# A graph-attention layer in fp32: the second projection with two levels of Strassen's scheme

## Chip, cores, metric

One core of one Trainium2 chip. Times are device microseconds of a whole execution. TensorE is PE in the profile, VectorE is DVE, ScalarE is ACT, GpSimd is POOL, and SP issues most transfers.

## The reference

128 graphs of 64 nodes with 512 features, all fp32: a norm with ReLU, a four-head graph attention, a second attention over the joined heads, a feed-forward network, a second norm and the residual.

```python
h = jnp.maximum(_layernorm(x), 0.0)
# attention 1: 4 heads, softmax over the neighbours, ELU; heads joined to 2048 features
h = elu(_gat_heads(h, adj, W_heads, a_heads));  h = transpose+reshape to [B, N, 2048]
# attention 2: the "second projection" is h @ W_out, 2048 -> 512
out = elu(_gat_heads(h, adj, W_out[None], a_out[None])[:, 0])
y = relu(out @ w1 + b1) @ w2 + b2 + out
return x + layernorm(y) * gamma + beta
```

## The kernel before

The 8192 rows go in 16 groups of four tiles of 128 rows. In each group TensorE does the first projection of one group (`g_a`, four heads), then its second projection (`g_b`), into which everything else is interleaved: the first attention of the next group (`pz`), the feed-forward products of the group before (`g_c` with w1, `g_d` with w2), transposes and scores. All four products use one level of Strassen's scheme in Winograd's form: seven products of half-size blocks instead of eight, numbered 1 to 7, which add up in three PSUM banks. A list scheduler fixes the order of each engine's instructions when the kernel is built; at run time each engine works through its own queue.

```python
ps = ctx.enter_context(tc.tile_pool(name="ps", bufs=6, space=PSUM))    # "mm" banks; 2 more for "aux"

def unit(name, product, post, order):
    own = {1: 1, 2: 1, 5: 5, 3: 5, 6: 6, 7: 6, 4: 6}       # which bank a product adds to
    def after(p):                                          # what happens when product p is done
        if p in (1, 5, 6):
            if p == 6:
                nc.vector.tensor_tensor(gb[6], gb[6], sb["s1"], ALU.add)
            nc.scalar.copy(sb[nm], gb[p])                  # s1, s5, t: copies of the banks
        elif p == 2: post("c11", gb[1])
        elif p == 7: post("c22", gb[6], sb["s5"], gb[1])
        elif p == 3: post("c12", gb[5], sb["t"], gb[5])
        else:        post("c21", gb[6])
    ...
```

So product 2 may start only when the copy s1 of product 1 is made, because it adds to the same bank; 7 waits in the same way for 6, and 4 for c22, which reads the bank after 7.

```python
def norm1(t):                                              # X[t] was loaded into another buffer
    mean, rstd = norm_stats(X[t], "n1", t)                 # VectorE, GpSimd
    HN[t] = big.tile([P, F], FP, tag="hn", name=f"hn{t}", bufs=G)
    nc.scalar.activation(HN[t], X.pop(t), AF.Relu, bias=nb, scale=rstd)

def project2(g):                                           # one level: 7 products x 4 heads x 4 matmuls
    ...
    return unit(f"b{g}", product_n(ms, lambda p, i: h1[slot[p]][:, i]), post, (1, 5, 6, 2, 7, 3, 4))

# first attention: two banks a task, one copied by ScalarE, one by VectorE
if b == 0: nc.scalar.copy(dst, srcv)
else:      nc.vector.tensor_copy(dst, srcv)

f1 = unit(f"c{g}", product_t(M1, ...), post1, (1, 5, 6, 2, 3, 7, 4))
f2 = unit(f"d{g}", product_n([M2], ...), post2, (1, 5, 6, 2, 3, 7, 4))
```

## Time and profile before

| | before |
|---|---|
| median of 3 (range) | 2364.44 us (2363.42 to 2364.57) |
| span of the profiled execution, mean granted clock | 2360.4 us, 0.992 |
| busy: TensorE, VectorE, ScalarE, GpSimd | 98%, 54%, 39%, 43% |
| distance of one group from the next (groups 1 to 13) | 143.0 us |

The distance is from the first `g_a` matmul of a group to that of the next. The lines themselves are in the prediction.

### The profile page before, as it was taken

The numbers are of one execution on the slowest core, as the hardware profiler recorded it, in microseconds if no ns is written. First come the engines' busy times: TensorE is split into PE (matmuls) and PEld (weight loads), VectorE is DVE, ScalarE is ACT, GpSimd is POOL, SyncE is SP. The second block draws the span as 40 slices with busy tenths as digits, with TensorE's granted clock in tenths as the row PEclk, the third lists the DMA queues.
The fourth block names the chain that finished last, engine by engine and source line by source line (L and its number), as shares of the span: only waits on it lengthen the run. The fifth ranks groups of instructions, "written<-read, shape, count | busy, mean of one in ns | idle before, by whom it ended". The sixth has DMA issues, their size and how long they took to land.

```text
span 2360.4 us, 32849 instructions
## 1 busy us (share of the span) xinstructions
PE 2317.9 (98%) x11805; PEld 1934.5 (82%) x11805; DVE 1265.5 (54%) x2210; ACT 911.0 (39%) x1623; POOL 1026.7 (43%) x917
## 2 busy tenths in 40 slices
PE   6989999999999999999999999999999999999997
PEld 4868787888878888787887878888788887878885
DVE  7625474554646556474554745556464563744527
ACT  2524425253352533425244251533525344251513
POOL 5664444416344353443524444253443534533333
PEclk7999999999999999999999999999999999999999
DMA  8545353444535445353444544435354453534443
GB/s 308 184 142 193 125 183 127 164 152 132 182 125 178 134 139 179 126 180 129 154 163 129 182 131 161 153 130 181 127 177 132 138 179 127 182 118 164 157 148 106
DMA packets 257809, 366.89 MB, mean 155 GB/s; under 512 B 22216, under 2 KB 145128, under 8 KB 257648
## 3 DMA queue, kind: packets, MB, share of 16 engines
q1 hardware_dynamic: 251024, 343.82, 43.9%
q0 software_dynamic: 4512, 16.78, 1.9%
q10 hardware_dynamic: 2112, 4.19, 0.5%
q8 instruction: 95, 1.56, 0.3%
q14 instruction: 66, 0.54, 0.1%
HBM read 337.45 MB, written 27.26 MB: 155 GB/s over the span
## 4 chain that ended last, share of the span: by engine, by line
PE 94%; DVE 2%; ACT 1%; POOL 1%; issue 0%; DMA 0%; DVEq 0%
PE g_b L322 33%; PE g_a L307 32%; PE g_c L307 8%; PE g_d L322 8%; PE pz L525 4%; PE pa L673 2%; PE pto L700 1%; PE pzS L525 1%; PE pth L371 1%; PE s1pt L472 1%; PE pf L381 1%; PE s1pe L406 1%; DMA x<-in_x_dram 0%; PE s2pt L667 0%; PE pwa L193 0%
## 5 line engine op out<-in xcount | busy, mean ns | idle before, releaser
L322 PE MATMUL g_b<-w,h 128*128 128x256 f32 x2560 | 598.1, 381 | 0.0
L322 PEld LDWEIGHTS g_b<-w,h 128*128 128x128 f32 x2560 | 480.5, 190 | 72.2 <-issue 10.1
L307 PE MATMUL g_a<-z,w 128*128 128x256 f32 x1520 | 361.0, 380 | 1.2 <-DVE g_a L581 0.7
L307 PE MATMUL g_a<-zs_z,w 128*128 128x256 f32 x1504 | 347.9, 379 | 0.0
L307 PEld LDWEIGHTS g_a<-z,w 128*128 128x128 f32 x1520 | 287.6, 190 | 57.9 <-issue 14.3
L307 PEld LDWEIGHTS g_a<-zs_z,w 128*128 128x128 f32 x1504 | 284.8, 190 | 50.5 <-issue 14.3
L322 PE MATMUL g_b<-w,hS 128*128 128x256 f32 x1024 | 243.5, 382 | 0.0
L585 POOL TENSOR_TENSOR hS<-hS,h 128x512 f32<-128x512 f32 x64 | 83.0, 1297 | 366.8 <-DVE hS L549 366.8
L547 ACT ACTIVATE exc<-g_a 128x512 f32<-128x512 f32 x256 | 152.3, 595 | 199.7 <-DVE g_a L581 119.6
L322 PEld LDWEIGHTS g_b<-w,hS 128*128 128x128 f32 x1024 | 191.4, 191 | 30.9 <-issue 6.7
L549 DVE SCALAR_TENSOR_TENSOR h<-exc,g_a 128x512 f32<-128x512 f32 x192 | 131.6, 686 | 136.3 <-ACT exc L548 136.2
L548 ACT ACTIVATE exc<-exc 128x512 f32<-128x512 f32 x256 | 161.6, 631 | 6.5
L615 POOL TENSOR_TENSOR h<-h,h 128x512 f32<-128x512 f32 x64 | 86.7, 1362 | 138.1 <-PE g_b L322 138.0
L332 POOL TENSOR_TENSOR zs_z<-zS,z 128x512 f32<-128x512 f32 x63 | 89.7, 1424 | 128.3 <-PE g_a L307 123.7
L615 POOL TENSOR_TENSOR h<-hS,h 128x512 f32<-128x512 f32 x64 | 81.1, 1268 | 142.4 <-PE g_b L322 142.4
L474 ACT COPY at<-s1pt 128x512 f32<-128x512 f32 x64 | 34.7, 588 | 279.8 <-PE s1pt L472 279.8
L307 PE MATMUL g_c<-ot,w 128*128 128x256 f32 x512 | 123.9, 385 | 0.8 <-DVE n2ve L347 0.8
L322 PE MATMUL g_d<-w,rt 128*128 128x256 f32 x512 | 121.5, 380 | 1.7 <-DVE o L740 1.0
L307 PE MATMUL g_a<-zS,w 128*128 128x256 f32 x496 | 117.2, 379 | 0.0
L639 DVE SCALAR_TENSOR_TENSOR jf<-wh,ao 128x512 f32<-128x512 f32 x128 | 94.3, 776 | 40.3 <-ACT wh L621 40.1
L333 POOL TENSOR_TENSOR zs_z<-z,zs_z 128x512 f32<-128x512 f32 x63 | 85.4, 1357 | 61.1 <-PE g_a L307 40.7
L307 PEld LDWEIGHTS g_c<-ot,w 128*128 128x128 f32 x512 | 93.9, 190 | 21.8 <-issue 9.3
(159 smaller groups left out, 3535.6 us busy)
## 6 DMA issues: line engine op xcount, KB each, us to landing
w<-tc SPq DMA_DIRECT2D x632, 256.0 KB, 2.6
w<-in_L_gnn_W_heads_dram SPq DMA_DIRECT2D x192, 256.0 KB, 2.7
w<-in_L_gnn_W_out_dram SPq DMA_DIRECT2D x192, 256.0 KB, 2.7
w<-in_L_gnn_w_dram SPq DMA_DIRECT2D x96, 256.0 KB, 2.7
x<-in_x_dram SPq DMA_DIRECT2D x66, 256.0 KB, 3.6
xr<-in_x_dram SPq DMA_DIRECT2D x64, 256.0 KB, 2.8
out_dram<-o SPq DMA_DIRECT2D x64, 256.0 KB, 2.1
tc<-pt POOLq DMA_DIRECT2D x20, 512.0 KB, 5.6
```

Source lines behind the costliest of these rows:

```text
L307: nc.tensor.matmul(bk[:, o, :], w[:, k, ts(o, P)], a[:, k, :], start=start and o == 0 and k == 0, stop=k == 1, skip_group_check=True,)
L322: nc.tensor.matmul(bk[:, j, :], a[:, k, ts(j, P)], w[:, k, :], start=start and k == 0 and j == 0, stop=i == len(ms) - 1 and k == 1, skip_g ...
L332: eng.tensor_tensor(s2, s1, a11, ALU.subtract)
L333: eng.tensor_tensor(s4, a12, s2, ALU.subtract)
L525: nc.tensor.matmul(banks[b][:, c, :].rearrange("p (h n) -> p h n", h=H), src[rows, off + c * P:off + (c + 1) * P], at[rows, b], start=True ...
L547: nc.scalar.activation(ex, src, AF.Relu, scale=-1.0)
L548: nc.scalar.activation(ex, ex, AF.Exp, scale=-1.0)
L549: nc.vector.scalar_tensor_tensor(dst, ex, -1.0, src, ALU.add, ALU.max)
L585: nc.gpsimd.tensor_tensor(dst, dst, H1["22"][:, h], ALU.add)
L615: nc.gpsimd.tensor_tensor(dst[:, h], x0[:, h], x1[:, h], ALU.subtract)
L639: nc.vector.scalar_tensor_tensor(junk, WH2[g][:, j], 1.0, ao[:, c, :], ALU.mult, ALU.mult, accum_out=f[:, c, j:j + 1],)
L673: nc.tensor.matmul(pa, AT2[g][:, j, :], WH2[g][:, j, :], start=True, stop=True)
```

## The change

Its intent: from the fourth group on (`DEEP = 3`, 13 of 16 groups), each of the seven block products of the second projection is itself done by Strassen's scheme, so TensorE does 49 quarter-size products where it did 28 pieces, an eighth less work. To pay for it, VectorE makes "quarter sums" of the activations, GpSimd makes the weights' second-level sums once ("block sums", groups 1 to 3), and the results keep seven blocks in two PSUM banks where one sufficed. To make room, x is normalized in its own buffer, buffers become single, the weight ring shrinks, the first attention leaves on ScalarE alone, and the feed-forward products get an order that holds fewer banks at once.

```diff
-    ring = ctx.enter_context(tc.tile_pool(name="ring", bufs=11))
+    ring = ctx.enter_context(tc.tile_pool(name="ring", bufs=10))
@@ load
-        tl = wk.tile([P, F], FP, tag="x", name=f"{name}{t}", bufs=4)
+        if name == "x":
+            tl = big.tile([P, F], FP, tag="hn", name=f"hn{t}", bufs=G)
         ...
@@ norm1
-        HN[t] = big.tile([P, F], FP, tag="hn", name=f"hn{t}", bufs=G)
-        nc.scalar.activation(HN[t], X.pop(t), AF.Relu, bias=nb, scale=rstd)
+        HN[t] = X.pop(t)
+        nc.scalar.activation(HN[t], HN[t], AF.Relu, bias=nb, scale=rstd)
@@ first attention
-                if b == 0:
+                if b == 0 or g > DEEP:
                     nc.scalar.copy(dst, srcv)
@@ weights of the second level, made on GpSimd during groups 1 to 3
+    def block_sums(p, i):
+        ... # two loads y, then
+        nc.gpsimd.tensor_tensor(t[:, 0], y12, y11, ALU.subtract)   # and three more
+        nc.gpsimd.dma_start(out=TQ[p][:, :, heads], in_=t)
@@ second projection, two levels
+        outer = (1, 2, 5, 6, 3, 7, 4)
+        halves = ((6, 7, 5), (3, 1, 2, 4))
+        def quarter_sums(p):
+            nc.vector.tensor_tensor(q2, x[:, :, 0, P:], x[:, :, 0, :P], ALU.subtract)
+            nc.vector.tensor_tensor(q3, x[:, :, 1, P:], q2, ALU.subtract)
+            nc.vector.tensor_tensor(q4, x[:, :, 1, :P], q2, ALU.subtract)
+        def part(p, half, j):
+                ...                               # cut: fetch of the weights, choice of the bank
+                if first:
+                    gb[p, half] = ps.tile([P, 4, P], FP, tag="mm", ...)
+                for h in range(H):
+                    nc.tensor.matmul(bk[:, place[j][1]], x[:, h], w[:, h], ...)   # 128 columns
+                if j == halves[half][-1]:
+                        after(p, half)            # eviction of this half (a wrapper is cut)
+                    if half == 1:
+                        if p == 3: inner(0, nc.gpsimd)
+                        if p == 4: inner(1, nc.vector)
+                if j == 3 and p != outer[-1]:
+                    quarter_sums(outer[outer.index(p) + 1])
@@ feed-forward
-        ... (1, 5, 6, 2, 3, 7, 4)
+        order = (1, 2, 5, 6, 3, 7, 4) if DEEP <= g + 1 < NG else (1, 5, 6, 2, 3, 7, 4)
```

## The prediction

> **What bounds the kernel now.** I read the page's first part and the chain that ended last, then the groups by form, then the timeline, then windows over one steady group of four row tiles.
>
> ```profile
> PE 2317.9 (98%) x11805; PEld 1934.5 (82%) x11805; DVE 1265.5 (54%) x2210; ACT 911.0 (39%) x1623; POOL 1026.7 (43%) x917
> ...
> PE 94%; DVE 2%; ACT 1%; POOL 1%; issue 0%; DMA 0%; DVEq 0%
> ```
>
> TensorE is busy 98% of the span and is 94% of the chain; its waits sum to some 35 us, nearly all in the first 130 us. No other engine passes 54%. So only work taken from TensorE shortens the kernel, and only while nothing else makes TensorE wait.
>
> The second projection is g_b. Its matmuls move 256 columns over 128x128 weights; each fp32 product is two records. The timeline gives their true spacing, the group its overlapped duration:
>
> ```profile
> 1013.77 1.89 PE L322 MATMUL g_b<-w,h 128*128 128x256 f32 x8
> 1015.50 1.89 PE L322 MATMUL g_d<-w,rt 128*128 128x256 f32 x8
> 1017.22 1.89 PE L322 MATMUL g_b<-w,hS 128*128 128x256 f32 x8
> ...
> 1041.39 1.04 PE L472 MATMUL s1pt<-ident,s1A 128*128 128x128 f32 x8
> ```
>
> Eight records every 1.726 us, so 215.7 ns a record. The nearest thing with 128 moving columns and a fresh 128x128 weight load each time is the transposes: eight in 1.04 us with a last record of 273 ns, so (1.04-0.273)/7 = 110 ns a record. Consecutive groups start 142.96 us apart (905.37, 1048.33). In windows over one of them (first projection; second projection up to the score projection pf; the rest of the second projection):
>
> ```profile
> 905.37:956.29 50.92, 50.92 (x231) 43.38 (x230) 27.38 (x52) 28.32 (x51) 11.70 (x9) 1.00 0.45 149
> 956.29:998.65 42.36, 42.36 (x258) 33.09 (x256) 16.71 (x23) 18.71 (x32) 24.98 (x25) 1.00 0.39 128
> 998.65:1048.33 49.68, 49.68 (x253) 43.25 (x250) 34.05 (x59) 9.68 (x19) 23.82 (x19) 1.00 0.53 174
> ```
>
> The columns are PE, PEld, DVE, ACT, POOL, clock, DMA share and GB/s. TensorE has no gap anywhere, but VectorE is unevenly loaded: 69% in the last stretch (both softmaxes, the feed-forward sums and evictions, the final norms), 39% in the middle one.
>
> **What the Trainium skill says.** "TensorE: Matmul & The Clock Gate", Back-to-back issue gap: a stream of weight load and matmul pairs is spaced by both, 81 ns at 128 columns against 56 ns for the matmul alone (its figures are for another type). The trace neither shows nor excludes such a loss for fp32: with 256 columns the 190 ns weight load hides, and transposes load weights in 141 ns. The same page, Part 1, says that the sequencer may spend about 62 ns on each matmul; the transposes at 110 ns do not show a limit, but they come in runs of 4 or 8 only. "SBUF — State Buffer", Who interferes with whom: a VectorE instruction with two SBUF inputs contends with a GpSimd instruction that reads SBUF, and the loser waits for the whole of the other. The trace agrees:
>
> ```profile
> 981.64 1.65 DVE L332 TENSOR_TENSOR zs_o<-ot,ot 128x512 f32<-128x512 f32 x1
> ...
> L332 DVE TENSOR_TENSOR zs_o<-ot,ot 128x512 f32<-128x512 f32 x16 | 26.4, 1652 | 0.6
> ...
> L332 DVE TENSOR_TENSOR zs_z<-zS,z 128x512 f32<-128x512 f32 x1 | 0.7, 710 | 0.1
> ```
>
> The same addition takes 0.71 us when GpSimd is quiet and 1.65 us beside GpSimd's sums.
>
> **The change, part by part.**
>
> *TensorE.* From the fourth group on (13 of 16) the 7 products x 4 heads x 4 matmuls of 256 columns (224 records) become 7 x 7 x 4 matmuls of 128 columns (392 records). Before: 224 x 215.7 ns = 48.3 us. After, at 109.5 ns, just under the transposes' spacing: 42.9 us. That is the ideal eighth less 0.8 us of record overhead: 5.4 us a group, 70 us in all, 3.0%. Everything else on TensorE stays.
>
> I take 109.5 because in the individual records the weight load of the next matmul starts 2 ns after a matmul starts, and a g_b matmul after a pause is recorded with 484 instead of 379 ns, so a weight load occupies about 105 ns: it just fits beneath 107 ns of streaming.
>
> *VectorE.* Added per deep group: 21 quarter sums of 512 elements with two SBUF inputs, 0.69 to 1.65 us, say 1.2: 25 us. Six evictions with an addition (384 or 512 elements, PSUM) in place of three: +1.7 us. The sums of one half of the result, five instructions with 1792 elements a row: about 4 us. Taken away: eight copies of the first attention at 0.687 us, 5.5 us. Net +25 us on 78 us, 103 of some 138 us: 75%, harmless as an average.
>
> *ScalarE.* +8 x 0.585 us of copies and +2.3 us of evictions on 57 us: under 50%. In the middle stretch it reaches about 25 of 40 us.
>
> *GpSimd.* Four sums at the end of the first projection (5.4 us) and one half of the inner sums (about 5 us) on 60.5 us. In groups 1 to 3 it also makes the 14 sets of weight sums, about 3 us each without their DMA waits; once only, and beside a first projection in which it has 39 us free.
>
> *x and norm.* The copy of x is not saved; only SBUF is. The load of x now waits for the last attention matmul that reads the buffer, in the middle of the weight queue. The norm has 30 us until its transposes, so I count nothing.
>
> *Where the gain is given back.* Stretch by stretch, the tightest is the last: after pf the compiled order leaves 28 small pieces at 0.876 us (24.5), 8 wide ones at 1.726 (13.8), scores and transposes (2.8): 41 us for TensorE instead of 49.7. VectorE has there its 34.05 us, plus nine quarter sums (products 3, 7 and 4) at 1.2 us, plus 1.7: 46.5 us. It does not fit. And the compiled order on VectorE puts the second softmax's weights (s1A) and their copy at the end of that list, behind the final norms and half of the score reductions, while TensorE needs them for the last two transposes, with only three small pieces and those transposes (3.5 us) behind. So TensorE arrives after about 37.5 us and VectorE is ready after 41 (quarter sums at 0.69) to 46 us (at 1.2): a wait of 4 to 8 us in each deep group. I take 4, as back-to-back VectorE instructions start some 0.07 us closer than their durations.
>
> A second, smaller wait stands at the start: the first small piece needs a quarter sum that follows ReLU, Exp, ELU and a GpSimd sum after the last head's first quadrant: 0.60+0.63+0.69+1.3+0.7 plus hand-overs, about 4.5 us, while TensorE has two wide products, 3.45 us. One us.
>
> Sum: 13 x (-5.4 + 4 + 1) = -5 us, nothing for the first three groups: about 2358 us.
>
> **Rivals.** (1) *The gain arrives.* If VectorE keeps up, 13 x 5.4 is saved, 2295 us; with 1.5 us of waits, 2315. For it: the kernel before shows no wait in 2200 us of this same style, and the evictions moved to ScalarE look meant to make room. Against: they make room in the middle stretch, not in the last. (2) *VectorE becomes the bound of the last stretch in full*: 8 us there and 2 at the start, 13 x 4.6 = +60, 2424 us. For it: the 46.5 against 41 us, and that blocked instructions block GpSimd too. (3) *Small matmuls cost more than 110 ns*: at 124 ns (sequencer or unhidden weight load) 392 x 14.5 ns eats the whole 5.4 us; with my waits 2430, without them 2365. (4) *Weights come too late*: 49 instead of 28 pieces of 256 KB, 21 of them in 512-byte rows. The hardware queue moved 343.82 MB with 43.9% of 16 engines' span, 0.79 us a piece, so it can just feed 0.876 us a piece; a ring of ten pieces holds 8.8 us instead of 11 x 1.73 = 19 us, and a final store in the same queue can hold it up. I give it about 1 us a group at most, because wide pieces and project-one pieces in between let it catch up.
>
> **Range and chances.** Gain and give-back are each about 5 us a group and I know the first far better than the second; 1 us of wait per group is 13 us, or 0.55%. Faster by over 2% needs under 1.8 us of waits in all; slower by over 2% needs over 9. That the change also reorders the feed-forward products and moves evictions suggests that waits were looked for, which keeps the chance of the first up. Range 2312 to 2412.
>
> **What would show it.** TensorE's small records at 109 to 111 ns apart (right) or over 115 (rival 3). Deep groups about 142.5 us apart; under 139, rival 1. TensorE waits on s1A in the list of waits, 4 us each, 13 times; on q at the start of the projection, 1 us each. Quarter sums with a mean near 1.2 us; VectorE over 90% busy after pf. Waits of TensorE for DMA would point to rival 4. I am wrong if the waits sum to under 20 us, or if the small matmuls are not near 110 ns.

## More of the kernel before

In a group of P us, I is the sum of TensorE's pauses (more than 20 ns between the end of a matmul's record and the start of the next). L is what the clock takes: half of the remaining time in stretches that the clock record shows at 0.5. W = P - I - L is TensorE's own work at full clock. Before, P = W = 143.0 and I = L = 0 in every steady group.

## The result, and the profile after

2570.76 us (2570.17 to 2572.65, 3 runs): 1.0876 times the time before, 95% interval 1.0851 to 1.0900. Ratios here and below are the mean time of one kernel's runs over that of the other's of the same rounds, so not quite the ratio of the medians. The prediction, 2358 us with a range to 2412, was wrong. The step that failed is its give-back: it allowed 5 us of waits in a group (4 on s1A, 1 at the start) and nothing for the groups before; measured were 10.6 us of waits and 6.1 us of half clock in a group, and 46 us in groups 0 to 2.

The page's first part and its chain, of the changed kernel:

```profile
PE 2361.8 (92%) x13989; PEld 2040.1 (79%) x13989; DVE 1522.6 (59%) x2491; ACT 973.8 (38%) x1784; POOL 1293.7 (50%) x1132
...
PE 63%; DVE 15%; POOL 13%; issue 6%; DMA 2%; ACT 1%; POOLq 0%; SPq 0%; DVEq 0%; ACTq 0%
```

Two things stand out. TensorE is the chain for 63% instead of 94%: it waits. And its busy time has *grown*, from 2317.9 to 2361.8 us, though an eighth of the second projection's arithmetic is gone: its clock was lower (0.955). The list of TensorE's waits (total us, times, longest):

```profile
PE g_d L380 <- DVE o L901: 62.4, 15, 8.7
PE pz L580 <- ACT z L590: 32.9, 11, 3.2
PE s1pt L530 <- DVE s1A L493: 18.5, 12, 5.4
PE s1pt L530 <- DVE s1A L497: 14.8, 13, 9.5
PE g_b L743 <- DVE wh L721: 10.8, 11, 1.1
PE g_b L743 <- PE g_a L365: 9.6, 13, 0.7
```

The groups lie 142.1, 166.8, 159.3, 158.2 and then 157.0 us apart, instead of 143.0 (the first 136.0). In a steady group with two levels P = 157.0 is W 140.3, I 10.6 and L 6.1. By the list, I is 3.8 us for c22 of d (the first row), 3.0 for z, 1.4 for s1A, 1.0 for `wh`, 0.7 at the start and 0.8 on GpSimd (`R`, the next row of the list, 8.4 us in all); what the first and fourth rows have beyond that fell mostly in groups 1 and 2. So 156 us of the 208 us by which the spans differ come from the 11 groups 3 to 13, 46 from groups 0 to 2, which have no second level yet, and the rest from the two ends.

One such wait, in TensorE's timeline of the changed kernel (start, length, instruction, and in brackets the pause before it with what ended it):

```profile
1129.37 1.06 PE L743 MATMUL g_b<-wq,q 128*128 128x128 f32 x8
1134.21 3.78 PE L380 MATMUL g_d<-w,rt 128*128 128x256 f32 x8 [3.78 <-DVE o L901]
1137.79 4.01 PE L743 MATMUL g_b<-wq,hS 128*128 128x128 f32 x24
```

The third line is 24 small records; where nothing disturbs, 24 take 2.84 us. The eight wide records of the second line take 3.78 instead of 1.89 us. This is half clock: product 4 of d waited 3.8 us for c22, and the clock record has a stretch of 6.8 us at 0.5, from 1133.4, so TensorE worked at half speed until 1140.2. VectorE's timeline shows why c22 (`o<-g_d`) was late:

```profile
1130.74 1.69 DVE L909 SCALAR_TENSOR_TENSOR o<-o,n2mv,gs 128x512 f32<-128x512 f32 x1
1132.35 1.21 DVE L690 TENSOR_TENSOR q<-h 128x512 f32<-128x512 f32 x1
1133.48 0.68 DVE L901 TENSOR_TENSOR o<-g_d,o 128x512 f32<-128x512 f32 x1
```

Product 7 had ended at 1127.6. From there to the sum VectorE was never idle: it had final norms, a sum of the second projection and a quarter sum in front of it, and the last two took 1.69 and 1.21 us where undisturbed ones take 0.74 and 0.69. The stretch from the score projection to the next group has, in the same columns as in the prediction:

```profile
1098.72:1152.62 53.90, 47.03 (x353) 43.08 (x353) 45.87 (x69) 9.48 (x19) 31.42 (x24) 0.94 0.66 196
```

VectorE (the third busy figure) works 45.9 us there; 46.5 was predicted. That is 85% of the stretch, which has itself grown to 53.9 us.

The second row of the waits, `pz` on ScalarE's copies of z, was not foreseen at all. ScalarE and then TensorE, changed kernel:

```profile
1070.72 0.81 ACT L417 ACTIVATE hn<-hn,n1nb,n1rs 128x512 f32<-128x512 f32 x1 [5.83 <-POOL n1nb L415]
1071.45 1.05 ACT L590 COPY z<-pz 128x512 f32<-128x512 f32 x2
```

```profile
1072.06 2.56 PE L580 MATMUL pz<-at,hn 64*128 64x256 f32 x8 [2.60 <-ACT z L590]
1074.55 2.07 PE L743 MATMUL g_b<-wq,q 128*128 128x128 f32 x8
```

ScalarE stood idle for 5.8 us with the norm of the next x at the head of its queue, while finished banks of z waited behind it. The norm needs `n1nb`, which GpSimd makes from the root `n1rs`. GpSimd:

```profile
1063.19 5.40 POOL L670 TENSOR_TENSOR h<-hS,h 128x512 f32<-128x512 f32 x4 [1.73 <-PE g_b L743]
1069.78 0.55 POOL L407 TENSOR_TENSOR n1rs<-n1ve,mhalf 128x1 f32<-128x1 f32 x1
```

x itself had landed by 1063.8 (VectorE's statistics start there) and the root's input was ready at 1064.9; the root stood behind GpSimd's sums for 4.9 us more. In the like waits of groups 3 to 13 it stood so for 3.2 to 5.2 us, in all but one of them. So the greater part of this wait was the order of GpSimd's queue, and not a late x. "TensorE: Matmul & The Clock Gate", section "Architectural detail: the array is 16× 32×32, not 1× 128×128", of the Trainium skill says that ScalarE's and VectorE's queues are strictly first in, first out; the trace agrees, with its 5.8 us.

And in groups 1 and 2, GpSimd (changed kernel):

```profile
330.17 1.33 POOL L391 TENSOR_TENSOR zs_z<-z,zs_z 128x512 f32<-128x512 f32 x1
334.41 0.72 POOL L280 TENSOR_TENSOR ty<-y 128x256 f32<-128x256 f32 x1 [2.91 <-DMA y<-tco]
335.09 0.72 POOL L282 TENSOR_TENSOR ty<-y 128x256 f32<-128x256 f32 x1
335.77 0.56 POOL L407 TENSOR_TENSOR n2rs<-n2ve,mhalf 128x1 f32<-128x1 f32 x1
```

The block sums had moved into the end of the second projection, and the final norm's root (`n2rs`) stood behind them and behind their wait for data. VectorE waited for the root (6.8 us before 336.4), TensorE for VectorE.

So the theory to test had four parts: (A1) waits at the head of in-order queues, (A2) too much work on VectorE in the last stretch, (A3) half clock after each longer pause, (A4) block sums on GpSimd. The rival: the small matmuls themselves, or the parts that every group shares.

### The profile page after: what moved, and what is told of

Same layout as the page of the kernel before. It is cut to its first block, busy times and chain, and to the rows that moved or that the text cites. A ratio compares the mean times of both kernels' runs of the same rounds, so it can differ in the third digit from the quotient of the medians.

```text
span 2568.1 us, 38627 instructions
## 1 busy us (share of the span) xinstructions
PE 2361.8 (92%) x13989; PEld 2040.1 (79%) x13989; DVE 1522.6 (59%) x2491; ACT 973.8 (38%) x1784; POOL 1293.7 (50%) x1132
## 4 chain that ended last, share of the span: by engine, by line
PE 63%; DVE 15%; POOL 13%; issue 6%; DMA 2%; ACT 1%; POOLq 0%; SPq 0%; DVEq 0%; ACTq 0%
PE g_a L365 29%; PE g_b L743 11%; PE g_c L365 7%; PE pz L580 4%; PE g_b L380 4%; POOL h L670 3%; DVE jf L797 2%; PE pa L832 2%; POOL o L901 1%; DVE n2st L401 1%; POOL zs_z L390 1%; PE pth L429 1%; DVE o L901 1%; DVE q L692 1%; PE g_d L380 1%
## 5 line engine op out<-in xcount | busy, mean ns | idle before, releaser
L743 PE MATMUL g_b<-wq,q 128*128 128x128 f32 x2184 | 306.4, 286 | 23.2 <-DVE wh L721 10.8
L743 PEld LDWEIGHTS g_b<-wq,q 128*128 128x128 f32 x2184 | 277.5, 198 | 55.0 <-issue 17.3
L743 PE MATMUL g_b<-wq,h 128*128 128x128 f32 x2080 | 265.9, 277 | 0.0
L743 PEld LDWEIGHTS g_b<-wq,h 128*128 128x128 f32 x2080 | 252.7, 192 | 15.5 <-issue 9.9
L602 ACT ACTIVATE exc<-g_a 128x512 f32<-128x512 f32 x256 | 152.4, 595 | 221.6 <-DVE g_a L636 139.9
L380 PEld LDWEIGHTS g_d<-w,rt 128*128 128x128 f32 x512 | 107.1, 219 | 85.3 <-DVE o L901 66.2
L580 PE MATMUL pz<-at,hn 64*128 64x256 f32 x768 | 132.9, 436 | 32.9 <-ACT z L590 32.9
L906 POOL TENSOR_TENSOR xr<-xr,bs 128x512 f32<-128x512 f32 x64 | 97.0, 1523 | 119.1 <-DMA xr<-in_x_dram 98.4
L670 POOL TENSOR_TENSOR hS<-h,h 128x512 f32<-128x512 f32 x64 | 86.4, 1376 | 119.1 <-PE g_b L743 112.1
L401 DVE BATCH_NORM_STATS2 n1st<-hn 128x6 f32<-128x512 f32 x64 | 44.4, 694 | 150.4 <-DMA hn<-in_x_dram 150.1
L580 PEld LDWEIGHTS pz<-at,hn 64*128 64x128 f32 x768 | 82.2, 203 | 57.5 <-ACT z L590 35.0
```

Of the source, the lines that this page charges most:

```text
L380: nc.tensor.matmul(bk[:, j, :], a[:, k, ts(j, P)], w[:, k, :], start=start and k == 0 and j == 0, stop=i == len(ms) - 1 and k == 1, skip_g ...
L401: nc.vector.bn_stats(st, src)
L580: nc.tensor.matmul(banks[b][:, c, :].rearrange("p (h n) -> p h n", h=H), src[rows, off + c * P:off + (c + 1) * P], at[rows, b], start=True ...
L602: nc.scalar.activation(ex, src, AF.Relu, scale=-1.0)
L670: nc.gpsimd.tensor_tensor(dst[:, h], x0[:, h], x1[:, h], ALU.subtract)
L743: nc.tensor.matmul(bk[:, place[j][1]], x[:, h], w[:, h], start=first and h == 0, stop=h == H - 1, skip_group_check=True,)
```

## The experiments

Eighteen kernels ran, four times each. P, W, I and L are means over groups 4 to 13, worked out as said above.

| run | what it is | time us | ratio to before (95%) | P | W | I | L |
|---|---|---|---|---|---|---|---|
| before | | 2364.4 | | 143.0 | 143.0 | 0 | 0 |
| after | the change | 2570.8 | 1.0876 (1.0851 to 1.0900) | 157.0 | 140.3 | 10.6 | 6.1 |
| level1 | one level everywhere, no block sums | 2443.9 | 1.0331 (1.0315 to 1.0346) | 149.2 | 142.8 | 4.3 | 2.1 |
| level1_blocks | the same, with block sums | 2485.8 | 1.0515 (1.0500 to 1.0531) | 149.3 | 142.8 | 4.3 | 2.2 |
| level1_order | level1, old feed-forward order | 2369.6 | 1.0018 (1.0001 to 1.0035) | 142.5 | 142.5 | 0 | 0 |
| level1_5banks | level1_order, five banks | 2402.1 | 1.0166 (1.0149 to 1.0183) | 144.7 | 143.6 | 1.1 | 0 |
| noq | after, 3 of 21 quarter sums | 2507.7 | 1.0611 (1.0592 to 1.0629) | 151.6 | 140.6 | 7.2 | 3.8 |
| norm_late | after, norm behind z's copies | 2528.7 | 1.0698 (1.0681 to 1.0716) | 152.8 | 140.3 | 9.2 | 3.3 |
| blocks_late | after, block sums behind the roots | 2545.1 | 1.0764 (1.0748 to 1.0780) | 157.0 | 140.3 | 10.5 | 6.2 |
| d743 | after, d as 1,2,5,6,7,3,4 | 2612.6 | 1.1050 (1.1033 to 1.1066) | 160.4 | 140.7 | 13.0 | 6.7 |
| best1 | d743 with the two repairs above it | 2549.5 | 1.0783 (1.0767 to 1.0800) | 157.0 | 140.5 | 11.1 | 5.5 |
| order_gap | after, d as 1,2,6,5,7,3,4 | 2541.3 | 1.0747 (1.0729 to 1.0765) | 154.0 | 140.7 | 9.3 | 4.0 |
| best2 | norm_late + blocks_late + order_gap | 2473.8 | 1.0460 (1.0436 to 1.0484) | 150.3 | 140.5 | 7.1 | 2.6 |
| best3 | best2, last transposes moved | 2476.7 | 1.0476 (1.0460 to 1.0491) | 149.9 | 140.8 | 7.3 | 1.7 |
| best3_noq | best3, 3 of 21 quarter sums | 2458.0 | 1.0394 (1.0379 to 1.0410) | 149.1 | 140.4 | 6.3 | 2.4 |
| best4 | best2, one ScalarE copy later | 2451.7 | 1.0362 (1.0345 to 1.0380) | 147.6 | 140.9 | 6.1 | 0.5 |
| best4_noq | best4, 3 of 21 quarter sums | 2473.4 | 1.0475 (1.0448 to 1.0503) | 150.6 | 140.5 | 7.5 | 2.6 |
| best5h | best4, two repairs more | 2464.2 | 1.0425 (1.0410 to 1.0441) | 148.5 | 139.9 | 6.4 | 2.2 |
| best6 | best5h, score reductions later | 2451.9 | 1.0373 (1.0357 to 1.0388) | 147.8 | 140.0 | 5.8 | 2.0 |
| best6_noq | best6, 3 of 21 quarter sums | 2406.6 | 1.0182 (1.0165 to 1.0199) | 144.0 | 140.3 | 3.5 | 0.2 |

The runs with few quarter sums have a wrong result (relative error 0.66). d743 and best1 have one by mistake.

### Which part costs what

**level1.** The second projection keeps one level, and the sums that serve only the second level go with it; nothing else of the change is undone.

```diff
-        second = project2_deep if g >= DEEP else project2
+        second = project2
-            if g <= DEEP:              # block sums
+            if False:
-            if g >= DEEP and h == H - 1:   # first-level sums for the quarter sums
+            if False:
```

> The second projection keeps one level of Strassen's scheme in all groups and the weight sums for the second level are not made; x in the norm's buffer, the ring of ten, the single buffers, the ScalarE evictions and the new feed-forward order stay. Theory A (three causes: VectorE overloaded by quarter sums, block sums on GpSimd, norm waiting for the late x in ScalarE's queue): the last cause alone remains, about 3 us of wait plus some 3 us of half clock in up to 14 groups, so 2400 to 2440 us, with TensorE waiting on z evicted by ScalarE. Rival B (all of the loss belongs to the second level): 2360 to 2370 us and no such wait. Rival C (the loss is in the shared parts): above 2500 us.

2443.9 us: somewhat above the range of theory A, but for a cause that it did not have. No wait of `pz` on z showed. The only large row in TensorE's waits of this run is

```profile
PE g_d L380 <- ACT s_d L331: 41.4, 12, 3.7
```

Product 2 of d waits for ScalarE's copy of product 1, which the new feed-forward order puts directly in front of it. Groups 0 to 2, with the old order, were 142.5 to 142.7 us apart, the others 148 to 150. So theory A was wrong about this run, and so were both rivals.

**level1_blocks.**

```diff
 level1, but:
-            if False:                  # block sums
+            if g <= DEEP:
```

> As the run with one level everywhere, but the fourteen sets of weight sums are made on GpSimd in groups 1 to 3 and never used. Theory A: about 40 us over that run, all of it in groups 1 and 2 (23.8 and 16.3 us over 143 us in the changed kernel), with TensorE waiting on VectorE's final norms, which wait for GpSimd. Rival (these groups lose their time to something else that the change brings at the start): within 8 us of the run with one level.

41.9 us over level1, with groups 1 and 2 at 168.4 and 160.6 us: as theory A said. The block sums cost about 42 us, though nothing uses them here.

**level1_order.**

```diff
 level1, and:
-        order = (1, 2, 5, 6, 3, 7, 4) if DEEP <= g + 1 < NG else (1, 5, 6, 2, 3, 7, 4)
+        order = (1, 5, 6, 2, 3, 7, 4)
```

> As the run with one level in all groups, but the two feed-forward products in their old order (1,5,6,2,3,7,4) too. In that run the first three groups, which still have the old order, were 142.5 us apart, and the others 148 to 150 us, with TensorE waiting 3.5 us on ScalarE's copy of product 1 before product 2 may add to the same bank. Theory A: only that order cost the 80 us, and x in the norm's buffer, the ring of ten and the ScalarE evictions cost nothing in this setting: 2360 to 2375 us, groups 142.5 to 143.5 us apart. Rival B (the shared parts cost something by themselves once z leaves on ScalarE, from the fourth group on): groups over 146 us, above 2410 us.

2369.6 us, 142.5 us apart, no wait in a steady group: theory A. x in the norm's buffer, the ring of ten, single buffers and ScalarE's evictions cost a steady group nothing under one level. The whole is 5 us slower than the kernel before, at the start: group 0 took 146.1 us instead of 136.0 in the profile. Whether the old order would also serve under two levels was not tried. The profile's first line is that of the kernel before, with VectorE lighter:

```profile
PE 2320.0 (98%) x11805; PEld 1942.3 (82%) x11805; DVE 1205.3 (51%) x2114; ACT 943.3 (40%) x1719; POOL 1027.9 (43%) x917
```

The pair level1 and level1_order also prices a pause. In one, TensorE pauses 4.3 us a group, 3.7 of it in one wait; the groups are 6.7 us longer. The difference is L, 2.1 us, and 0.3 of W. This is part A3.

**blocks_late.**

```diff
-        nc.gpsimd.tensor_tensor(t[:, 0], y12, y11, ALU.subtract)
+        first = nc.gpsimd.tensor_tensor(t[:, 0], y12, y11, ALU.subtract)
+        # first depends on the last root (n2rs) of the final norm that was issued
```

> The changed kernel, but each set of weight sums on GpSimd has to stay behind the last of the final norm's reciprocal roots issued before it, so the sums and their wait for data no longer stand in front of it. Theory A (the loss of groups 1 and 2 is this queue order, not the amount of work): 2525 to 2540 us, groups 1 and 2 below 150 us. Rival B (the amount of work or the buffers shared with the feed-forward cost it): above 2555 us, groups 1 and 2 above 155 us.

26 us less than the changed kernel, groups 1 and 2 at 148.2 and 147.3 us instead of 166.8 and 159.3. The time lies just above theory A's range, the groups within it. So 26 of the 42 us of the block sums were the order of GpSimd's queue; part A4 holds in that form. Group 3 took 3.6 us more.

### The waits of the two-level groups

**norm_late.**

```diff
-        nc.scalar.activation(HN[t], HN[t], AF.Relu, bias=nb, scale=rstd)
+        act = nc.scalar.activation(HN[t], HN[t], AF.Relu, bias=nb, scale=rstd)
+        # act depends on ScalarE's last copy of z of this attention
```

> The norm's ReLU on ScalarE is made to stay behind the last copy of z of the attention that frees its buffer, so that it never waits for its x in front of those copies. Everything else as in the changed kernel. Theory A: the wait of TensorE on z (3.1 us in each deep group) and the window of half clock after it go, 11 to 14 groups of 5 to 6.5 us, so 2485 to 2515 us, and groups about 151 us apart. Rival B (VectorE is the real limit and the wait only moves to its next hand-over): 2550 to 2571 us, with the waits on d's c22 and on s1A grown by about what z's wait lost.

2528.7 us: 42 us less than the changed kernel, 4.2 a group, where 5 to 6.5 was expected, and outside both ranges; the wait on z is gone from the list. Part of the gain is taken back: the wait on VectorE's sum of the two-level product 7 (`wh`, which the texts call c21's sums) grew from 10.8 to 20.5 us in all.

**noq.**

```diff
-                    quarter_sums(outer[outer.index(p) + 1])
+                    QS[outer[outer.index(p) + 1]] = QS[p]
```

> Wrong result on purpose: the three quarter sums are made for the first product of each second projection only, and the other six products use those again. TensorE's work, the small matmuls, the block sums, the norm and the evictions are unchanged; VectorE loses 18 of 21 quarter sums a deep group, about 20 us. Theory A (VectorE's queue is overloaded in the last stretch): the waits on d's c22, on s1A and on the second half of c21's sums and the half clock after them go, about 5.8 us of waits and 3.2 us of half clock in 13 groups, so 2430 to 2470 us. Rival B (small matmuls or the clock alone, not VectorE): within 20 us of 2571.

2507.7 us, 63 us less, 5.4 a group: VectorE's load matters (rival B is out), but theory A expected 100 to 140 us. The wait on c22 did not go:

```profile
PE g_d L380 <- DVE o L901: 52.2, 26, 8.6
```

It became 2.7 us instead of 3.8 in each group, with a second one of 0.2. VectorE now waited for GpSimd in front of c22 (1.1 us for a root, 2.3 us for a sum of o), so quantity was not the whole of it. The scheduler also set some of VectorE's other instructions in another order.

**d743** and **best1**, a mistake.

```diff
-        f2 = unit(f"d{g}", ..., post2, order)
+        last = (1, 2, 5, 6, 7, 3, 4) if DEEP <= g + 1 < NG else order
+        f2 = unit(f"d{g}", ..., post2, last)
```

> The changed kernel with one line added: in the last feed-forward product (d) of the groups with two levels, product 3 stands between product 7 and product 4, so that VectorE has one wide product and two or three small pieces more, about 4 us, to read product 7's bank before product 4 may add to it. Theory A (this one hand-over costs 3.8 us of wait and about 3.1 us of half clock in each of 12 groups): 2485 to 2510 us, groups about 151 us apart. Rival B (VectorE is short of time in the whole last stretch, so the wait moves to s1A or to the sums of c21): 2540 to 2575 us, with these waits grown by some 3 us a group.

> The three repairs at once: weight sums behind the final norm's roots, the first norm behind the last copy of z, product 3 between products 7 and 4 of d. If they add up (42 us measured for the norm, some 40 for the weight sums, some 75 for d's order): about 2410 us, deep groups near 145 us. Rival (VectorE is the limit of the last stretch and takes back what one repair gives): deep groups at 149 us or more, 2460 us or more.

2612.6 and 2549.5 us, with wrong results (relative error 0.22): by the code the final norm of the first tile is issued after the fifth product of d, which was no longer product 3, so it read rows that were not complete. Their times tell one thing. Product 7 now stood directly behind 6, and TensorE waited 4.3 us in 11 groups for ScalarE's copy t of the bank, a wait that was not there before. In level1, where 2 stands directly behind 1, the like wait was 3.7 us.

**order_gap**, the repaired form.

```diff
+        turned = (1, 2, 6, 5, 7, 3, 4) if DEEP <= g + 1 < NG else order
+        f2 = unit(f"d{g}", ..., post2, turned)
 # and the first tile's final norm comes after the sixth product, the second's after the seventh
```

> The repaired form of the run with product 3 between products 7 and 4, whose result was wrong because the first final norms were then issued ahead of product 3, and whose product 7 stood directly behind product 6 and waited 4.3 us for ScalarE's copy of it. Here d's order is 1,2,6,5,7,3,4 in the groups with two levels: at least one wide product between 6 and 7 and between 7 and 4; the final norms of the first two tiles come behind product 3. Theory A (d's hand-over of one bank from product 7 to 4 costs 3.8 us of wait and some 3 us of half clock in each deep group): deep groups 150 to 152 us apart, 2480 to 2510 us. Rival B (VectorE is short in the whole last stretch and the wait only moves to s1A or to the sums of c21): 154 to 157 us apart, 2535 to 2571 us.

2541.3 us, 154.0 us apart: 3.0 us a group. By the numbers this is rival B, at the edge of its range. By the mechanism it is neither: the wait on c22 went from the two-level groups, and one of 3.9 us in 11 groups took its place, not on VectorE but of product 2 on ScalarE's copy of product 1 (44.9 us in all).

**best2**, the three repairs together.

> Three repairs at once: weight sums behind the final norm's roots (alone 2545), the first norm behind the last copy of z (alone 2529), d's new order. If they add up: 2571 - 26 - 42 - 75 = 2428 us, deep groups about 147 us apart. Rival B (VectorE is the limit of the last stretch): deep groups about 152 us, 2500 us.

2473.8 us, between the 2428 and the 2500 of the two theories. The three gains add up: 2570.8 - 42.1 - 25.7 - 29.5 = 2473.5. So these repairs neither help nor hinder each other; order_gap was only worth less than I had thought.

**best3.**

```diff
+        if DEEP <= g < NG - 2:          # the last two transposes of the weights s1A
+            held, turns = turns[-1:], turns[:-1] + [nothing]     # go to the next group
```

> As the run with three repairs, and the last two transposes of the first attention's weights are moved from the end of the second projection into the next group's first projection, so that TensorE no longer needs VectorE's softmax to be ready at the end. If VectorE's queue is only late, not short over the whole group (its busy share is 59%), this takes the waits on s1A away, 1.2 us and what follows, and deep groups come to 142 to 146 us: 2370 to 2410 us. Rival B (VectorE's arrears go on into the next group and return as waits on the first projection's evictions): deep groups stay within 1.5 us of the run with three repairs.

2476.7 us, no gain: rival B. The waits on s1A went (1.2 us a group), and TensorE paused in the first projection instead, 13.0 us in all for nothing that the profile names ("issue") and 9.3 for VectorE's sums of `g_a`.

**best3_noq.** The same with the edit of noq.

> Wrong result on purpose: the run before this with the quarter sums of the first product used for all seven, so VectorE makes 3 of 21. It asks what the two-level projection is worth when nothing waits for its sums. Theory A (TensorE's own saving of 3 to 5 us a group is real): deep groups 138 to 141 us, 2310 to 2350 us, below the kernel before. Rival C (the small matmuls give TensorE nothing, whatever VectorE does): deep groups at 142.5 us or more, 2364 us or more.

149.1 us apart, which by the number is rival C. It does not speak for C, since W is 140.4; the groups are long because the wait on ScalarE's copy s_d was still there, 4.4 us in each of 11 groups (49.8 us in all). ScalarE's timeline, in best3, shows what stood in front of that copy:

```profile
1221.55 0.48 ACT L729 COPY wh<-g_b 128x384 f32<-128x384 f32 x1 [9.73 <-DVE g_b L728]
1221.93 0.59 ACT L337 COPY s_d<-g_d 128x512 f32<-128x512 f32 x1
```

The copy of the two-level product 6 waits for a VectorE sum, and ScalarE idles 9.7 us with it at the head.

**best4**, from best2.

```diff
+                copy = nc.scalar.copy(home(0, 1), bk)    # two-level product 6, issued half a product later
+                # copy depends on ScalarE's copy s_d of d's product 1
```

> The run with three repairs (2474 us, TensorE waiting 3.5 to 3.9 us on ScalarE's copy of d's product 1 in each group with two levels), with ScalarE's copy of the two-level product 6 put behind that copy. Theory A (one more copy that waits for VectorE at the head of ScalarE's queue): that wait falls below 1 us and the half clock after it goes, 5.5 to 6.5 us in 12 or 13 groups, so 2390 to 2410 us, deep groups 143 to 145 us apart. Rival B (VectorE is short of time and the wait moves to another hand-over): 148 us or more, above 2450 us.

2451.7 us: 22 us, 2.7 a group, where 6 was expected; theory A failed, and rival B's numbers are met almost (147.6 us apart instead of 148). The wait on s_d went, L fell to 0.5, and two smaller waits came: 2.0 us on VectorE's sum of c11 and 1.0 on t_d. The 1.3 us on s1A were there before.

**best4_noq.**

> Wrong result on purpose: the run before this with the quarter sums of the first product used for all seven. Theory A: TensorE's own work is 139.8 to 140.3 us a deep group by its records (143.0 before), so with nearly no waits 140 to 142 us apart and 2335 to 2365 us; then quarter sums cost the difference to the run before this, 2 to 3 us a group. Rival C (the small matmuls save TensorE nothing): 143 us or more and 2375 us or more.

It took longer than best4. By the number that is rival C again, but W is 140.5, and it answers nothing on quarter sums: with other instructions the scheduler set another head of the queue, the first softmax's Exp.

```profile
1213.21 0.63 ACT L498 ACTIVATE s1e<-s1e 128x512 f32<-128x512 f32 x1 [10.26 <-DVE s1e L497]
1213.75 0.57 ACT L337 COPY s_d<-g_d 128x512 f32<-128x512 f32 x1
```

### Banks, and order against quantity

**level1_5banks**, from level1_order.

```diff
-    ps = ctx.enter_context(tc.tile_pool(name="ps", bufs=6, space=bass.MemoryType.PSUM))
+    ps = ctx.enter_context(tc.tile_pool(name="ps", bufs=5, space=bass.MemoryType.PSUM))
```

> The run with one level and the old order (2370 us, groups 142.5 us apart, no waits), with five PSUM banks instead of six for the products. Theory D (the two-level form waits because its results hold twice the banks, so every eviction's lateness reaches TensorE): waits of TensorE on z, s_d or o appear, groups 146 us or more, above 2420 us. Rival A (banks are not short, only the queues are late): groups within 1 us of 142.5, below 2390 us.

2402.1 us, 144.7 us apart. "PSUM — Partial Sum Buffer", "Specifications (TRN2)", of the Trainium skill gives 8 banks of 512 fp32 values a partition; six serve the products here. With five, TensorE waits a little:

```profile
PE g_d L380 <- ACT wh L779: 9.6, 13, 0.7
...
PE pzS L580 <- ACT z L590: 4.2, 14, 1.0
```

Waits of theory D's kind appear, but at 2.2 us a group, half of them in W, not the 3.5 that it asked for; the result lies between the two theories. So the banks that the second level takes are a contribution, and a small one as far as one bank shows; that two banks would do more was not tried.

**best5h**, from best4.

```diff
-        A = sm.tile([P, 2, H + 1, N], FP, tag=w + "A", ..., bufs=1)
+        A = sm.tile([P, 2, H + 1, N], FP, tag=w + "A", ..., bufs=2)
-        halves = ((6, 7, 5), (3, 1, 2, 4))
+        halves = ((5, 6, 7), (1, 2, 4, 3))       # and half 1 before half 0
-                if j == 3 and p != outer[-1]:    # place of the next quarter sums
+                if j == 7 and p != outer[-1]:
-    ring ... bufs=10
+    ring ... bufs=8
```

> The run with four repairs (2452 us; per deep group 140.9 us of TensorE work, 6.1 us of waits, 0.5 us lost at half clock), with a second buffer for the first softmax's weights, so that the last ones need not wait for the transposes of those before (1.8 us of wait), the half that needs no quarter sums first in each product (0.7 us of wait at the start), and a ring of eight for room. If the waits go and none comes in their place: groups 144 to 145 us apart, 2410 to 2425 us. If VectorE's arrears move to the next hand-over: 147 us, 2450 us. If a ring of eight is too small, TensorE waits for weights by DMA.

2464.2 us, 12 us more than best4 and above both forecasts (2425 and 2450). The waits on s1A and at the start went, and all of it and more came back in one place, 5.4 us in each group on VectorE's sum of the two-level product 7 (`wh L739`), which reads the bank that product 4 adds to. TensorE did not wait for weights in this run, so a ring of eight was enough here.

**best6** and **best6_noq**.

```diff
+            red = nc.vector.scalar_tensor_tensor(...)     # score reductions of the second attention
+            # red depends on VectorE's last instruction of the final norm
```

> The run with six repairs (2464 us; 139.9 us of TensorE work, 6.4 us of waits, 2.2 us lost at half clock a group), with the score reductions on VectorE held behind the last final norm, so they no longer wait for GpSimd's inner sums in front of the sums of c21. Theory A1 (order of queues): the 5.4 us wait falls below 2 us, groups 141.5 to 144 us apart, 2375 to 2410 us. Theory A2 (quantity of VectorE's work): the wait stays or moves, groups 147 us or more, 2450 us or more.

> Wrong result on purpose: the run before this with the quarter sums of the first product used for all seven. Theory A1: within 1 us a group of that run. Theory A2: at least 4 us a group less, 140 to 143 us apart. If it falls to 140 to 141 us, the two-level projection by itself is worth some 2 us a group against one level (142.5), 2340 to 2360 us.

2451.9 us (147.8 us apart) and 2406.6 us (144.0). The long wait in the lists of TensorE, first best6, then best6_noq:

```profile
PE g_b L761 <- DVE wh L739: 51.7, 12, 4.7
```

```profile
PE g_b L761 <- DVE wh L739: 12.0, 11, 1.1
...
PE g_a L371 <- DMA w<-tc: 11.5, 9, 1.6
```

Theory A2 gives 147 or more for best6, and without the quarter sums at least 4 us less, 140 to 143; measured 147.8, 3.8 less, and 144.0. So it is met in the first and missed by a little in the second, while A1 asked for under 1 us. A rival is that the scheduler moved other instructions too, as in best4_noq. In a steady group (the one that starts with `g_a` of group 7), leaving the quarter sums out, 127 of 134 instructions of VectorE, 112 of 114 of ScalarE and 60 of 62 of GpSimd stand in the same order in both runs, so this pair differs by the quarter sums and by little else. The 3.8 us are rather too low: in best6_noq a new wait appears, 1.8 us a group on weights, most of it in the first projection. Whether its ring of eight is the cause was not tried. The windows from the score projection to the next group, again with VectorE as the third busy figure, for level1_order, best6 and best6_noq:

```profile
1157.06:1202.88 45.82, 45.79 (x257) 39.40 (x257) 34.66 (x57) 7.88 (x16) 24.04 (x19) 1.00 0.55 170
```

```profile
1193.40:1244.41 51.01, 45.91 (x361) 43.02 (x361) 44.43 (x67) 9.56 (x19) 26.89 (x22) 0.97 0.66 198
```

```profile
1172.21:1221.02 48.81, 46.13 (x361) 43.03 (x361) 34.77 (x59) 9.49 (x19) 25.39 (x22) 0.97 0.69 207
```

One level leaves VectorE at 34.7 us of 45.8. Two levels put 44.4 us on it, and with its own waits for ScalarE and GpSimd that no longer fits beside TensorE. Without 18 quarter sums VectorE is back at 34.8 us and the long wait is 1.1 us. Even then the kernel is 42 us slower than the kernel before. In the profiles (38 us) 20 us of it lie in groups 0 to 2, where the block sums are made, 12 in groups 3 to 13, whose waits of 3.5 us a group outweigh the gain in W, and 6 at the ends.

No version beat the kernel before, so none is offered as better.

## Why the prediction was wrong, point by point

The sum was 13 x (-5.4 + 4 + 1) = -5 us. Measured, a two-level group was not 0.4 us shorter but 14.0 us longer (-2.7 of W, 10.6 of waits, 6.1 of clock), and the groups before added 46 us that the sum did not have. Its main suspect, VectorE in the last stretch, was right; the path by which the waits reach TensorE, and most of their size, were not, and two queues and the clock were left out.

- **TensorE's gain, "5.4 us a group": the mechanism right, the size off.** W fell from 143.0 to 140.3, and against one level in the same surroundings from 142.5: a gain of 2.2 to 2.7 us. The mis-sized term is "392 at 109.5 ns". Small records follow each other at 112 ns, and with the pieces' seams at 114.2 ns on average (wide ones at 217.5), so 392 x 114.2 = 44.8 us against 224 x 217.5 = 48.7 us: 3.9 us. Another part goes at the seams with the attention: from each record to the next, `pz` took 7.0 us in a group of best4, 6.4 in one of the kernel before and 6.1 in one of level1_order. Which switches cause this was not tried. Rival 3 (124 ns) did not come true.
- **"A wait of 4 to 8 us in each deep group; I take 4" for s1A: the cause right, the place and the size off.** VectorE was overloaded in the last stretch as worked out (45.9 us measured, 46.5 predicted). But TensorE met it earlier, at product 4 of d (3.8 us) and at the two-level product 4 (1.0), and for s1A only 1.4 us. I looked for one hand-over at the end of VectorE's list, and there were three along it. best5h and best6 show that the same lack comes out wherever the order leaves it.
- **"1 us at the start": right**, 0.7 us, 13 times. The list puts it down to TensorE's own `g_a`, but the timeline has the first small piece start at 1047.6, just as VectorE ends the quarter sum that it reads (1047.5).
- **"The norm has 30 us until its transposes, so I count nothing": wrong.** The norm itself was in time. What I did not ask is what stands behind it in ScalarE's queue (copies that free banks), and what stands in front of its root in GpSimd's (four sums, 5.4 us). It cost 42 us (norm_late).
- **Block sums "once only, and beside a first projection in which it has 39 us free": wrong.** They did not stay in the first projection. They cost 42 us (level1_blocks), most of it by standing in front of the final norm's roots (blocks_late).
- **What the sum left out: the clock.** A pause was counted by its length. L is 6.1 us a group, so a wait of 10.6 us cost 16.7. I cited the page that describes the gate and did not use it, since the kernel before has no pauses.
- **Rival 2 (VectorE as the bound, 2424 us)** had the right cause and missed the factor of the clock and the two queue effects. **Rival 1** fails with W. **Rival 4** (weights too late) was not seen in the changed kernel: no wait of TensorE on weights in its two-level groups appears in the list, and a ring of eight still sufficed in best5h. Waits on weights show where VectorE no longer holds TensorE up: 1.8 us a group in best6_noq.
- **Small slips of its sums**, which decide nothing: the record overhead is 0.65 us and not 0.8 (6.04 - 5.39); 34.05 + 9 x 0.69 + 1.7 is 42 us and not 41, so by its own figures the wait was 4.5 to 9 us, not 4 to 8; and 2364.4 - 5.2 is 2359. Quarter sums came to 1.04 us on average and 1.27 in the last stretch (1.2 was assumed).

How the 206 us divide, by the runs: order of GpSimd's queue 26 (blocks_late), norm in front of z's copies 42 (norm_late), d's order 29 (order_gap), one ScalarE copy 22 (best2 to best4), quarter sums 45 (best6 to best6_noq), and 42 left in best6_noq. The 45 are rather too low, because of the waits on weights in best6_noq. These are steps of one path; in another order the shares would differ, as the first noq, with 63 us, shows. What stays open: how much of the remaining 42 us is banks or the ring of eight, and whether an arrangement exists in which VectorE's quarter sums fit. If all waits could be removed, W alone would give 13 x 2.2 = 29 us under level1_order, some 2341 us (an estimate from the table), so by this estimate over 2% was not to be had.

## What to carry to other kernels

When one engine has no slack, price a change by what it adds to the *other* engines in the very stretch where it adds it, and then walk along each of their queues: an instruction that waits at the head holds up everything behind it, however idle the engine is on average. When a repair only moves a wait, the engine behind it may be short of time (best6) or there may be one more instruction at the head of a queue (order_gap, whose new wait best4 took away); take the work away once, even at the price of a wrong result, and check that the order stayed the same, to tell the two apart. And count TensorE pauses by their length too: here pauses with one or two of 3 to 4 us among them cost about one and a half times their sum (10.6 us took 6.1 more in the changed kernel, 4.3 took 2.1 in level1), pauses of at most 2.0 us little more than their sum (6.1 took 0.5 in best4).

## What the Trainium skill lacked or had wrong

- "TensorE: Matmul & The Clock Gate", Part 1: it sets the fall to half clock at one idle window, about 3.4 us, and warns of pauses over some 3 us (of shorter "micro-idles" it says that they can do it too, without a length). Shorter ones did it here. Of pauses over 0.5 us that stood alone (no other over 0.5 us within 8 us), counted over groups 1 to 13 of the twenty profiles: up to 1.25 us, none of 358 was followed by half clock; from 1.25 to 2.25 us, 17 of 47; from 2.25 to 3.25 us, 61 of 74; longer, 175 of 179. (Ends of matmuls are modelled, so the lengths are good to some 0.1 us.)
- The same part says that one busy window of about 3.4 us releases the clock. The half-clock stretches inside these runs lasted 3.4 us or, mostly in the changed kernel, 6.8 us (a few of them about 10); the page prices the throttled time, at half of it as L does here, but not a pause of a given length. Here pauses of 4.3 us a group, 3.7 of them in one wait, cost 6.7 us (level1 against level1_order).
- "TensorE: Matmul & The Clock Gate", Back-to-back issue gap: it has no figure for fp32 ("FP8 and Floating Point Precision" counts passes, without a time). Measured: 112 ns a record with 128 columns and a fresh weight load each, 216 ns with 256 columns, at full clock, two records to a product.
- No page gives a time for a switch between matmuls of different shapes ("TensorEngine Tiling (Array Packing)" says that a change of the tiling mode drains TensorE, without a figure). Within a run of attention matmuls (64 rows) the two records of a product start 7 ns apart and the next product starts mostly 209 ns after the second; a second-projection record in its place starts 306 ns after it.
